# Second cross-attention: queries and keys of four heads in even and odd tiles, scores in eight parts of TensorE

## The chip, the cores and the metric

The kernel runs on one core of a Trainium2 chip. The metric is the device time in microseconds (us) of one execution. The kernel before has a median of 2383.0 us in three runs (2380.41 to 2383.2).

## The reference, cut to what matters

Two transformer blocks work on `x` (8 batches, 512 rows, 256 columns), all in float32. The change lies in the cross-attention of the second block, where 512 rows of a batch ask 64 context rows, with 16 heads of width 64:

```python
def _attn(xq, ctx, wq, wkv, wo, bo):
    q = _heads(xq @ wq)                       # 16 heads, 512 x 64 each
    k, v = jnp.split(ctx @ wkv, 2, axis=-1)   # 16 heads, 64 x 64 each
    k = _heads(k); v = _heads(v)
    q = _rope(q, sq, cq)                      # (even, odd) -> (even*c - odd*s, even*s + odd*c)
    k = _rope(k, sk, ck)
    sim = jnp.einsum('bhnd,bhmd->bhnm', q, k) * DH ** (-0.5)
    a = jax.nn.softmax(sim, axis=-1)
    o = jnp.einsum('bhnm,bhmd->bhnd', a, v)
    return o.transpose(0, 2, 1, 3).reshape(...) @ wo + bo
```

Before it come the first block (a self-attention, a cross-attention and a gated feed-forward) and the second block's self-attention over 512 rows; after it comes the second block's feed-forward.

## The kernel before, in words

The program runs in stages: the first block (three batches' pieces interleaved by `run_blocks`, a planner that places work by slots), the second block's self-attention (`slots`, pool `ph4`), the second cross-attention (`cross`, pool `ph5`) and the last feed-forward (`feed_forward`). In the last three the order on TensorE (PE), VectorE (DVE), ScalarE (ACT) and GpSimd (POOL) is the order in which the Python code issues the instructions. The DMAs of SyncE's queue (SP) are put in order by the scheduler, so their place can differ from the code's.

**Keys and values.** The keys of the second cross-attention are made during the first block: `keys1(p)` multiplies, rotates with `rope_pair` (L844 on) and `store_keys1` writes one pair of heads to the DRAM tile `k_d` by a DMA that POOL issues. Values come at the end of the self-attention stage (`cross_values`). Per batch, `load_kb` and `load_vb` fetch them to one of two sets of SBUF tiles. A tile `kb` is `[128, 8 pairs, 2, 64]`: it holds each pair of heads twice as wide as needed, the half that belongs to the other head being zero, so that one matmul with 128 rows gives the scores of two heads.

**Rope.** `rope_pair` takes a PSUM tile that holds two heads, with even and odd components in blocks of 32 partitions. DVE does one product with the cosine over 128 partitions (L849) and two with the sine over 64 partitions each, which land exchanged (L852). One POOL addition makes the turned tile `q` (L853).

**The stage around the change.** `cross` walks 8 batches `b` of 8 steps `j`. A step issues one pair's query product and rope (`queries`, three ahead: `LEAD = 3`). Steps 0, 2, 4 and 6 issue `score(b, j // 2)`: two matmuls of 128x128 weights by 512 columns into one two-bank PSUM tile `ps_S`, and one exponential of 1024 columns on ACT (L1261) that makes a tile `p` of two pairs. `sums` multiplies four pairs of `p` by a 128x32 selector[...]. ACT copies the sums (L1271), and a round trip through DRAM (L1274, L1276) lays them out for a reciprocal on DVE (`inverse`, L1281). Its result goes back through DRAM (L1283), and eight DMAs spread it over partitions as `rb` (L1288). `scaled` multiplies the four pairs of one half of the heads by `rb`, even pairs on POOL and odd ones on DVE (L1295). `outer` multiplies values with the output weights into `vw`, and `cross_out(b - 1, t)` multiplies the scaled `p` of the batch before with `vw`, pair 0 to pair 7 in that order, for rows of tile `t`. `turn` transposes the rows of the next batch, and `rows_` normalises those of the one after. PSUM tiles of `queries`, `outer`, `sums`, `turn` and `cross_out` come from one ring of four banks (`bank_x`: `D`, `O`, `X`, `X`).

**Form of matmuls.** A float32 matmul shows as two records in the trace. Where a helper issues a matmul, its line is L118. The self-attention's `score` (L1019 on) already uses heads in fours: even and odd components of four heads are in two tiles, each head having 32 partitions[...].

Of the kernel before, what the change touches and what calls it, by code (L numbers as in the profile page):

```python
# [10 lines left out]
F32 = mybir.dt.float32  # L11
# [7 lines left out]
P = 128  # L19
# [68 lines left out]
def fast_path(ctx: ExitStack, tc: tile.TileContext, a: dict, out: bass.AP):  # L88
# [28 lines left out]
    def mm(o, lhsT, rhs, start=True, stop=True):  # L117
        nc.tensor.matmul(o, lhsT, rhs, start=start, stop=stop)  # L118
# [144 lines left out]
    def load_k(dst, src, p=P):  # L263
        nc.sync.dma_start(dst, src.rearrange("(k p) f -> p k f", p=p))
# [223 lines left out]
    def at(i, fn):  # L488
        beside.setdefault(max(i, -1), []).append(fn)
# [348 lines left out]

    k_d = dram.tile([P, NPAIR, B, T], F32, name="k_d", bufs=1)
    v_d = dram.tile([P, NPAIR, B, T], F32, name="v_d", bufs=1)

    def rope_pair(wk, ps, c, sn, shape, dst):  # L844

        t1 = wk.tile([P, N], F32, tag="t1", name="t1")
        t2 = wk.tile([P, N], F32, tag="t2", name="t2")
        t1, t2 = (t[:, :].rearrange("p (j n) -> p j n", n=shape[-1]) for t in (t1, t2))
        nc.vector.tensor_tensor(t1, ps, c.to_broadcast(shape), ALU.mult)  # L849
        for i in range(2):  # L850
            src, d = slice(64 * i, 64 * i + 64), slice(64 - 64 * i, 128 - 64 * i)
            nc.vector.tensor_tensor(t2[d], ps[src], sn[src].to_broadcast([64, *shape[1:]]), ALU.mult)  # L852
        nc.gpsimd.tensor_tensor(dst, t1, t2, ALU.add)  # L853

    kv1_stack = ExitStack()
    kv1 = {}
# [1 line left out]
    def open_keys1():  # L858
        kv1["pool"] = pool = kv1_stack.enter_context(tc.tile_pool(name="kv1", bufs=2))
        kv1["w"] = w = pool.tile([96, 2, H * HD1], F32, name="w_ck", bufs=1)  # L860
        load_k(w, a["ca_wk2"], 96)
        for n in ("rope_c", "rope_s2"):
            kv1[n] = t = pool.tile([P, T], F32, name=f"t_{n}", bufs=1)
            nc.sync.dma_start(t, a[n][:, 0:T])

    def keys1(p):
        ps = bank_x()
        for k in range(2):
            mm(ps, kv1["w"][:, k, p * P : (p + 1) * P], ctxzT[:, k, :], k == 0, k == 1)
        kv1[p] = q = kv1["pool"].tile([P, N], F32, tag="q", name="q", bufs=8)  # L870
        rope_pair(kv1["pool"], ps.rearrange("p (j n) -> p j n", j=B), kv1["rope_c"][:, None, :], kv1["rope_s2"][:, None, :],
                  [P, B, T], q.rearrange("p (j n) -> p j n", j=B))

    def store_keys1(p):
        nc.gpsimd.dma_start(k_d[:, p], kv1[p].rearrange("p (b t) -> p b t", b=B))

    wk2 = wk3 = w_1 = w_3 = w_2 = None
    wpool = nk = rope_c = rope_s = w_sq = w_sk = w_sv = w_so = ready = None
# [42 lines left out]
    at(CYCLE, open_cross)  # L921
    for p in range(NPAIR):
        at(CYCLE + 2 + 2 * p, lambda p=p: keys1(p))
        at(min(CYCLE + 5 + 2 * p, 2 * CYCLE), lambda p=p: store_keys1(p))
    at(2 * CYCLE, open_ff)
    at(CYCLE * B + X1 + 3, open_block1)
    for n in range(3):
# [15 lines left out]
    kvs = []  # L943

    def kv_first():
        w = wpool.tile([P, 2, NPAIR, 2, T], F32, tag="w4", name="kv", bufs=1)
        kvs.append((w[:, 0], w[:, 1]))
        return kvs[0]

    def load_kb(b):  # L950
        for i in range(4):
            r = slice(32 * i, 32 * i + 32)
            nc.sync.dma_start(kvs[b % 2][0][r, :, i % 2, :], k_d[r, :, b, :])

    def load_vb(b):
        for e in range(2):
# [1 line left out]
            nc.sync.dma_start(kvs[b % 2][1][r, :, e, :], v_d[r, :, b, :])  # L958

    def cross_weights():  # L960
        cross.update(v=load_w("ca_wvp", 1, 96), o=load_w("ca_wo", 2), q=load_w("ca_wq2", 0),
                     s=load_table("rope_s2", "s"))

    def cross_values(wk, p):
        ps = bank_x()
# [7 lines left out]
    with tc.tile_pool(name="ph4", bufs=2) as wk:  # L973
# [8 lines left out]
        def batch4(b):  # L982
# [115 lines left out]
            if b:  # L1098

                pieces = normed_in_pieces(nk, b, EPS1, lambda z: s.update(z=z))  # L1100
                last(base - 8, pieces[0])
                last(base - 6, pieces[1])
                after[base - 6] = [pieces[2]]
                last(base - 5, lambda: add_row(b, row("sabo")))
                after.setdefault(base - 4, []).append(turn)
                last(base - 3, lambda: queries(0))
                last(base - 2, lambda: values(0, (0, 1)))
                last(base - 2, lambda: keys(0))
                last(base - 1, lambda: values(0, (2, 3)))
            else:  # L1110
                s["hT"] = ready

                def begin():
                    queries(0)
                    add_row(0, row("sabo"))
                    both = bank_s()
                    keys(0, (both[:, 0, :], both[:, 1, :]))
                    values(0, (0, 1))

                last(-1, begin)  # L1120

                after[-1] = [lambda: values(0, (2, 3))]
                last(4, lambda: [nc.gpsimd.memset(z, 0.0) for z in (kb, vb)])
                last(5, lambda: load_kb(0))
            for h in range(2):
                last(base + h, lambda h=h: values(1, (2 * h, 2 * h + 1)))
# [70 lines left out]
        with tc.manual_schedule(engines={ENG.PE, ENG.DVE, ENG.Activation, ENG.Pool}):  # L1197
            slots()

    w_co, w_cq, rope_s2, ready = cross["o"], cross["q"], cross["s"], first_rows[1]  # L1200

# [1 line left out]
    with tc.tile_pool(name="ph5", bufs=2) as wk:  # L1205
        w_f1 = load_w("ff_w1", 1)
        w_f2 = load_w("ff_w2", 3)
        kvs.append(tuple(wk.tile([P, NPAIR, 2, T], F32, name=n, bufs=1) for n in ("kb", "vb")))


        turned_rows = {0: ready, 1: first_rows[2]}
# [30 lines left out]
            nc.scalar.copy(s["vw"][:, 2 * pp : 2 * pp + 2, :], ps.rearrange("p (i d) -> p i d", i=2))  # L1242

        def queries(n):
            b, p = divmod(n, NPAIR)
            if b == B:
                return
            ps = bank_x()
            for k in range(2):
                mm(ps, w_cq[:, k, p * P : (p + 1) * P], turned_rows[b][:, k, :], k == 0, k == 1)  # L1250
            ss[b][p] = q = wk.tile([P, N], F32, tag="q", name="q", bufs=7)
            rope_pair(wk, ps[:, None, :], rope_c[:, None, :], rope_s2[:, None, :], [P, 1, N], q[:, None, :])

        def score(b, pp):
            s = ss[b]
            ps = bank_s()
            for i in range(2):
                p = 2 * pp + i
                mm(ps[:, i, :], kvs[b % 2][0][:, p, :, :].rearrange("p e k -> p (e k)"), s[p])
            s["p", pp] = pr = wk.tile([P, 2, N], F32, tag="p", name="p", bufs=8)  # L1260
            nc.scalar.activation(pr, ps, AF.Exp, scale=HD1 ** -0.5)  # L1261

        def sums(b, half):

# [86 lines left out]
            return good  # L1351

        def cross():
            LEAD = 3
            for n in range(LEAD):
                queries(n)
                if n:
                    outer(0, n - 1)
            for z in kvs[1]:
                nc.gpsimd.memset(z, 0.0)  # L1360
            for b in range(B):
                for j in range(NPAIR):
                    if j % 2 == 0:
                        queries(NPAIR * b + j + LEAD)
                        score(b, j // 2)
                    if b and j in (5, 6):
                        cross_out(b - 1, j - 4)
                    if j % 2:
                        queries(NPAIR * b + j + LEAD)
                    if j < 2:  # L1370
                        for pp in (2 * j, 2 * j + 1) if b else (2 + j,):
                            outer(b, pp)
                    if b:
                        if j == 0:
                            scaled(b - 1, 0)
                        if j == 1:
                            inverse(b - 1, 1)
                        if j == 3:
                            scaled(b - 1, 1)
                    if j == 3:  # L1380
                        turn(b + 1)
                    if b:
                        if j == 7:
                            cross_out(b - 1, 3)
                    if j == 2 and b + 1 < B:
                        load_kb(b + 1)
                        load_vb(b + 1)
                    if j == 4:
                        sums(b, 0)
                        if b:  # L1390
                            cross_out(b - 1, 0)
                    if j > 4:
                        rows_(b + 2, j - 5)
                    if j == 6:
                        inverse(b, 0)
                    if j == 7:
                        sums(b, 1)

        def feed_forward():
            good = top = None  # L1400
# [803 lines left out]
def _layout(inputs):  # L2204
# [24 lines left out]

    arr["ca_wv"] = l1["ca_wkv"][:, H * HD1 :].reshape(CD, 8, 2, HD1).transpose(0, 2, 1, 3).reshape(CD, H * HD1)  # L2230

    def both_apart(w):
        return w.reshape(w.shape[0], NPAIR, 2, HD1 // 2, 2).transpose(0, 1, 4, 2, 3).reshape(w.shape[0], H * HD1)

    arr["ca_wq2"], arr["ca_wk2"] = both_apart(l1["ca_wq"]), both_apart(l1["ca_wkv"][:, : H * HD1])
    def fours(w):
        return w.reshape(w.shape[0], H // 4, 4, HD1 // 2, 2).transpose(0, 1, 4, 2, 3).reshape(w.shape[0], H * HD1)

    arr["sa_wq4"], arr["sa_wk4"] = fours(l1["sa_wq"]), fours(l1["sa_wkv"][:, : H * HD1])
    arr["ca_wvp"] = l1["ca_wkv"][:, H * HD1 :]  # L2240

    cols = np.zeros((P, NCOL), f)

# [23 lines left out]
    arr["rope_c"] = np.concatenate([cos] * 4, axis=0)  # L2267
    arr["rope_s"] = np.concatenate([sin, -sin] * 2, axis=0)
    arr["rope_s4"] = np.concatenate([sin] * 4, axis=0)
    arr["rope_s2"] = np.concatenate([sin, sin, -sin, -sin], axis=0)  # L2270
    return {k: np.ascontiguousarray(v, dtype=f) for k, v in arr.items()}


# [14 lines left out]
```

## Time and profile before

| What | Value |
|---|---|
| median of three runs | 2383.0 us |
| span of the profiled execution | 2378.6 us |
| PE busy in it | 2361.7 us, 99% of the span |
| DVE, ACT, POOL busy | 1141.8, 886.8, 958.6 us |
| second cross-attention, from its first query product to the last feed-forward's first matmul | 1815.4 to 2131.9 us of the span |
| PE stretches of its batches 2 to 5 | 41.13 us each |

Busy times are sums over one engine, idle time is what is left, and the wait shown with an instruction is the idle time of its engine just before it. The profiled execution's span is 4.4 us less than the median of the three runs: that is what lies around the first and last instruction, and run-to-run spread. On a timeline of PE, the records of one matmul start about 0.43 us apart where they have 512 columns. The shown length of a group is longer by the modelled end of its last record, so the distance between two starts is read, not the length.

### The profile page before, as it was taken

The page shows a single profiled execution, that of the slowest core. Times are in us where ns is not written, and L with a number is a line of the kernel's source. Part 1 is how long each engine was busy: PE and PEld are TensorE (multiplying, and loading weights), DVE is VectorE, ACT ScalarE, POOL GpSimd, SP SyncE. Part 2 cuts the span into 40 slices and gives each one's busy share as a digit, 9 for nine tenths or more (in the row PEclk, how much of TensorE's full clock was granted, in tenths as well). Part 3 has the DMA queues.
Part 4 walks back from the last instruction along what each step waited for, and adds up shares of the span by engine and source line. Part 5 has one row for each costly group of instructions (what it writes and reads, how often), then busy time and mean ns, then how long its engine had stood idle before and what let it go on. Part 6 is the DMA issues. An engine that isn't in the chain of part 4 may idle for free.

```text
span 2378.6 us, 28548 instructions
## 1 busy us (share of the span) xinstructions
PE 2361.7 (99%) x10964; PEld 1153.9 (49%) x10964; DVE 1141.8 (48%) x2115; ACT 886.8 (37%) x1118; POOL 958.6 (40%) x588
## 2 busy tenths in 40 slices
PE   9999999999999999999999999999999999999999
PEld 4333544544545633434444444444345566667666
DVE  4564544534335345555454555545445767651110
ACT  4665545555542134333333333333332222221221
POOL 4563223323201046555555555555543545441110
PEclk9999999999999999999999999999999999999999
DMA  5130000000002001000000000000123222210000
GB/s 186 38 104 11 17 15 13 16 15 6 13 11 93 1 1 33 10 26 12 19 19 19 19 19 20 19 19 19 37 59 103 74 65 69 65 59 28 18 23 20
DMA packets 84897, 84.07 MB, mean 35 GB/s; under 512 B 42656, under 2 KB 59792, under 8 KB 84752
## 3 DMA queue, kind: packets, MB, share of 16 engines
q1 hardware_dynamic: 83208, 78.99, 10.8%
q8 instruction: 88, 1.44, 0.2%
q0 software_dynamic: 640, 2.10, 0.2%
q10 hardware_dynamic: 904, 1.07, 0.1%
q14 instruction: 57, 0.47, 0.1%
HBM read 72.09 MB, written 10.04 MB: 35 GB/s over the span
## 4 chain that ended last, share of the span: by engine, by line
PE 96%; DMA 1%; DVE 1%; issue 1%; ACT 1%; POOL 0%; SPq 0%; DVEq 0%; ACTq 0%; POOLq 0%
PE ps_X L118 39%; PE ps_S L118 24%; PE ps_D L118 16%; PE ps_O L118 14%; PE ps_X L429 1%; DMA rb<-rec 1%; PE ps_X L616 1%; PE ps_X L576 0%; ACT p L596 0%; DMA rec<-rec 0%; PE ps_D L616 0%; PE ps_D L429 0%; POOL var L567 0%; PE ps_D L576 0%; ACT den L1063 0%
## 5 line engine op out<-in xcount | busy, mean ns | idle before, releaser
L118 PE MATMUL ps_S<-q,k 32*128 32x512 f32 (+1 forms) x3072 | 416.3, 622 | 2.5 <-ACT p L596 1.5
L1028 ACT ACTIVATE p<-ps_S 128x1024 f32<-128x1024 f32 x256 | 248.4, 1021 | 449.5 <-PE ps_S L118 449.2
L596 ACT ACTIVATE p<-ps_S 128x1024 f32<-128x1024 f32 x256 | 248.2, 1022 | 197.5 <-PE ps_S L118 196.8
L118 PEld LDWEIGHTS ps_S<-q,k 32*128 32x128 f32 (+1 forms) x3072 | 141.5, 183 | 228.0 <-issue 161.5
L1047 DVE TENSOR_TENSOR sm<-sm,p 128x1024 f32<-128x1024 f32 x128 | 251.8, 2026 | 0.3 <-issue 0.2
L1010 POOL TENSOR_TENSOR q<-t 128x512 f32<-128x512 f32 x32 | 59.7, 1866 | 327.8 <-DVE t L1008 286.8
L1007 DVE TENSOR_TENSOR t<-ps_X,rope_c 128x512 f32<-128x512 f32 x126 | 86.9, 690 | 211.2 <-PE ps_X L118 211.2
L184 POOL TENSOR_TENSOR rstd<-rstd,mhalf 128x4 f32<-128x4 f32 x49 | 50.1, 1023 | 329.4 <-DVE rstd L183 328.1
L853 POOL TENSOR_TENSOR q<-t,t 128x512 f32<-128x512 f32 x72 | 94.9, 1318 | 154.8 <-DVE t L852 151.7
L567 POOL TENSOR_TENSOR var<-var,mhalf 128x32 f32<-128x32 f32 (+1 forms) x17 | 87.4, 5140 | 170.1 <-DVE var L561 169.9
L1043 POOL TENSOR_TENSOR sm<-p 128x1024 f32<-128x1024 f32 x64 | 149.9, 2370 | 1.8 <-ACT p L1028 1.8
L118 PE MATMUL ps_X<-hT,w 128*128 128x512 f32 x328 | 150.5, 597 | 0.0
L1093 POOL TENSOR_TENSOR oT<-oT,rb 128x512 f32<-128x512 f32 x63 | 126.7, 2029 | 29.2 <-DMA rb<-rec_d 29.2
L118 PE MATMUL ps_O<-p,v 128*64 128x512 f32 x512 | 134.9, 605 | 0.0
L118 PE MATMUL ps_D<-p,v 128*64 128x512 f32 x512 | 131.6, 592 | 0.0
L118 PE MATMUL ps_O<-p,h 128*32 128x512 f32 x1024 | 130.4, 610 | 0.8 <-ACT p L596 0.8
L118 PE MATMUL ps_X<-w_sa_wv,hT 128*128 128x512 f32 x256 | 118.3, 605 | 0.0
L118 PE MATMUL ps_X<-hT,w_sa_wq 128*128 128x512 f32 x256 | 115.9, 595 | 0.0
L118 PE MATMUL ps_X<-w_sa_wo,oT 128*128 128x256 f32 x512 | 113.9, 381 | 0.6 <-DVE t L1008 0.5
L118 PE MATMUL ps_X<-hT,w_sa_wk 128*128 128x512 f32 x248 | 113.2, 599 | 0.0
L118 PE MATMUL ps_S<-hT,w_ff_w 128*128 128x512 f32 x256 | 111.3, 592 | 0.0
L466 DVE TENSOR_TENSOR x<-ps_X,x 128x512 f32<-128x512 f32 x27 | 18.7, 691 | 190.5 <-PE ps_X L118 190.5
(283 smaller groups left out, 3619.4 us busy)
## 6 DMA issues: line engine op xcount, KB each, us to landing
rb<-rec SPq DMA_DIRECT2D x128, 128.0 KB
rb<-rec_d SPq DMA_DIRECT2D x124, 128.0 KB
rb<-rec SPq DMA_DIRECT2D x16, 256.0 KB
out_dram<-x SPq DMA_DIRECT2D x15, 256.0 KB
x<-in_x_dram SPq DMA_DIRECT2D x7, 512.0 KB
gate<-modd SPq DMA_DIRECT2D x24, 128.0 KB
k_d<-q POOLq DMA_DIRECT2D x8, 256.0 KB, 2.4
v_d<-v SPq DMA_DIRECT2D x8, 256.0 KB
```

The source lines that it names most:

```text
L118: nc.tensor.matmul(o, lhsT, rhs, start=start, stop=stop)
L184: nc.gpsimd.tensor_tensor(r[:, :n], r[:, :n], mhalf[:, :n], ALU.pow)
L429: nc.tensor.transpose(ps[:, t * P : (t + 1) * P], z[:, t, k * P : (k + 1) * P], ident)
L567: nc.gpsimd.tensor_tensor(var, var, half, ALU.pow)
L596: nc.scalar.activation(pr[u], pss[u], AF.Exp, scale=HD0 ** -0.5)
L853: nc.gpsimd.tensor_tensor(dst, t1, t2, ALU.add)
L1007: nc.vector.tensor_tensor(c, ps, rope_c, ALU.mult)
L1010: nc.gpsimd.tensor_tensor(r[0], ec, os, ALU.subtract)
L1028: nc.scalar.activation(pr, pss[u], AF.Exp, scale=HD1 ** -0.5)
L1043: nc.gpsimd.tensor_tensor(sm, s["p", g, 0, u], s["p", g, 1, u], ALU.add)
L1047: nc.vector.tensor_tensor(s["sm", g, u], s["sm", g, u], s["p", g, t, u], ALU.add)
L1093: eng.tensor_tensor(o, o, s["rb", g, u], ALU.mult)
```

## The change

Queries and keys are now made for four heads at a time. For each group `g` of four heads there are an even and an odd product (`e`), each with its 32 components of four heads in 128 partitions. `rope_half` does two DVE products over 128 partitions for each; after the odd one, POOL makes the two turned tiles by a subtraction and an addition. `kb` has half the size, no zeros, and takes one DMA in place of four. `score(b, half)` takes eight heads at once: sixteen matmuls of 32 rows and 64 weight columns in four row by two column parts, into two `ps_S` tiles, followed by two exponentials. A tile column of `p` now holds two heads that are four places apart, and value and output weights are reordered to match. The order of `cross` is changed: `LEAD` is 5; scores come at steps 0 and 4; the sums of a half come right ahead of the scores of the next; `turn`, `inverse(b - 1, 1)` and `scaled(b - 1, 1)` move to steps 2, 2 and 4, and the four `cross_out` of a batch to steps 5, 6 and 7. The buffers of the rope's products (`t`) are five, those of `q` eight.

```diff
-    def rope_pair(wk, ps, c, sn, shape, dst):
...
-        nc.vector.tensor_tensor(t1, ps, c.to_broadcast(shape), ALU.mult)
-        for i in range(2):
-            src, d = slice(64 * i, 64 * i + 64), slice(64 - 64 * i, 128 - 64 * i)
-            nc.vector.tensor_tensor(t2[d], ps[src], sn[src].to_broadcast([64, *shape[1:]]), ALU.mult)
-        nc.gpsimd.tensor_tensor(dst, t1, t2, ALU.add)
+    def rope_half(pool, s, key, e, ps, c, sn, shape, bufs, dst):
...
+        s["t", key, e] = tc_, ts = tile(), tile()
+        nc.vector.tensor_tensor(shaped(tc_), ps, c.to_broadcast(shape), ALU.mult)
+        nc.vector.tensor_tensor(shaped(ts), ps, sn.to_broadcast(shape), ALU.mult)
+        if e:
+            (ec, es), (oc, os) = s.pop(("t", key, 0)), s.pop(("t", key, 1))
+            d = dst()
+            nc.gpsimd.tensor_tensor(d[0], ec, os, ALU.subtract)
+            nc.gpsimd.tensor_tensor(d[1], es, oc, ALU.add)
...
-    def store_keys1(p):
-        nc.gpsimd.dma_start(k_d[:, p], kv1[p].rearrange("p (b t) -> p b t", b=B))
+    def store_keys1(g):
+        nc.gpsimd.dma_start(k_d[:, g], kv1[g].rearrange("p e (b t) -> p e b t", b=B))
...
-        for i in range(4):
-            r = slice(32 * i, 32 * i + 32)
-            nc.sync.dma_start(kvs[b % 2][0][r, :, i % 2, :], k_d[r, :, b, :])
+        nc.sync.dma_start(kvs[b % 2][0], k_d[:, :, :, b, :].rearrange("p g e t -> p (g e) t"))
...
-        def score(b, pp):
+            rope_half(wk, ss[b], g, e, ps[:, None, :], rope_c[:, None, :], rope_s[:, None, :], [P, 1, N], 5, dst)
+
+        def score(b, half):
             s = ss[b]
-            ps = bank_s()
-            for i in range(2):
-                p = 2 * pp + i
-                mm(ps[:, i, :], kvs[b % 2][0][:, p, :, :].rearrange("p e k -> p (e k)"), s[p])
-            s["p", pp] = pr = wk.tile([P, 2, N], F32, tag="p", name="p", bufs=8)
-            nc.scalar.activation(pr, ps, AF.Exp, scale=HD1 ** -0.5)
+            pss = [bank_s() for _ in range(2)]
+            for e in range(2):
+                for j in range(4):
+                    r = slice(32 * j, 32 * j + 32)
+                    for i in range(2):
+                        g = 2 * half + i
+                        mm(pss[j // 2][64 * i : 64 * i + 64, j % 2, :], kvs[b % 2][0][r, 2 * g + e, :], s[g][e][r, :],
+                           e == 0, e == 1)
+            for u in range(2):
+                s["p", 2 * half + u] = pr = wk.tile([P, 2, N], F32, tag="p", name="p", bufs=8)
+                nc.scalar.activation(pr, pss[u], AF.Exp, scale=HD1 ** -0.5)
...
         def cross():
-            LEAD = 3
+            LEAD = 5
...
                 for j in range(NPAIR):
-                    if j % 2 == 0:
-                        queries(NPAIR * b + j + LEAD)
-                        score(b, j // 2)
-                    if b and j in (5, 6):
-                        cross_out(b - 1, j - 4)
-                    if j % 2:
-                        queries(NPAIR * b + j + LEAD)
-                    if j < 2:
-                        for pp in (2 * j, 2 * j + 1) if b else (2 + j,):
+                    if j == 0 and b:
+                        sums(b - 1, 1)
+                    if j == 4:
+                        sums(b, 0)
+                    if j % 4 == 0:
+                        score(b, j // 4)
+                    if j == 2:
+                        turn(b + 1)
+                    queries(NPAIR * b + j + LEAD)
+                    if b and j < 2:
+                        for pp in (2 * j, 2 * j + 1):
                             outer(b, pp)
                     if b:
                         if j == 0:
                             scaled(b - 1, 0)
-                        if j == 1:
+                        if j == 2:
                             inverse(b - 1, 1)
-                        if j == 3:
+                        if j == 4:
                             scaled(b - 1, 1)
-                    if j == 3:
-                        turn(b + 1)
-                    if b:
-                        if j == 7:
-                            cross_out(b - 1, 3)
+                        if j > 4:
+                            for t in ((0,), (1,), (2, 3))[j - 5]:
+                                cross_out(b - 1, t)
...
-                    if j == 4:
-                        sums(b, 0)
-                        if b:
-                            cross_out(b - 1, 0)
...
-                    if j == 7:
-                        sums(b, 1)
+            sums(B - 1, 1)
```

## The prediction

> **What bounds the kernel now.** I read the page first: busy time, then the chain of work that ended last.
>
> ```profile
> PE 2361.7 (99%) x10964; PEld 1153.9 (49%) x10964; DVE 1141.8 (48%) x2115; ACT 886.8 (37%) x1118; POOL 958.6 (40%) x588
> ...
> PE 96%; DMA 1%; DVE 1%; issue 1%; ACT 1%; POOL 0%; SPq 0%; DVEq 0%; ACTq 0%; POOLq 0%
> ```
>
> PE sets the end nearly alone. A change pays if it takes PE time away without making PE wait. The view by windows says the same of the changed stage; each window is one batch of the cross-attention:
>
> ```profile
> 1931.35:1972.48 41.13, 41.13 (x156) 25.30 (x152) 26.77 (x50) 8.94 (x12) 19.74 (x14) 1.00 0.24 68
> 1972.48:2013.61 41.13, 41.13 (x156) 25.30 (x152) 27.95 (x50) 8.94 (x12) 19.76 (x14) 1.00 0.23 67
> ```
>
> Columns: length, then busy time of PE, weight loads, DVE, ACT and POOL. PE never idles, though DVE and POOL are far from full. The timeline of PE in the second of them gives the prices (start, length, records):
>
> ```profile
> 1972.48 1.99 PE L118 MATMUL ps_X<-hT,w_ca_wq 128*128 128x512 f32 x4
> 1974.30 1.88 PE L118 MATMUL ps_S<-q,kv 128*128 128x512 f32 x4
> 1976.02 1.03 PE L118 MATMUL ps_X<-w_ca_wo,kv 128*128 128x256 f32 x4
> ...
> 1988.93 1.88 PE L118 MATMUL ps_S<-q,kv 128*128 128x512 f32 x4
> 1990.74 1.07 PE L118 MATMUL ps_O<-p,sel 128*32 128x512 f32 x8
> 1991.74 0.48 PE L118 MATMUL ps_X<-vw,p 128*128 128x256 f32 x1
> ```
>
> A score of four heads runs from 1974.30 to 1976.02: 1.72 us, four records at 0.43. The self-attention's scores show what row parts do:
>
> ```profile
> 1506.12 1.03 PE L118 MATMUL ps_D<-p,v 128*64 128x512 f32 x4
> 1507.08 2.00 PE L118 MATMUL ps_S<-q,k 32*128 32x512 f32 x16
> 1509.01 3.27 PE L118 MATMUL ps_X<-hT,w_sa_wk 128*128 128x512 f32 x7
> ```
>
> Sixteen records take 1.93 us: four rounds of four side by side, 4 x 0.43 = 1.72, and 0.21 for entering and leaving the form. The first line's four records need 0.86, two at a time, so column parts overlap too.
>
> [...] in the third fence the sums' two rounds (0.86) start 0.09 late (1988.93 + 1.72 = 1990.65), last 1.00, and the matmul after them is 0.10 longer (1.98 where 1.88 is usual), 0.33 in all. Eight parts at once appear in no row of before. [...] POOL's rope addition takes 1.26 alone, 1.71 beside DVE's scaling.
>
> **The change part by part.** Units are us; all sums are against the profiled span.
>
> *Scores.* Per half batch, before: two groups, 2 x 1.72 = 3.43. After: 16 matmuls, 32 records; in eight parts four rounds, 1.72. Sixteen halves: 16 x 1.716 = **27.5 less**. If only the four row parts overlap, it is eight rounds and nothing is saved.
>
> *Mode changes.* Before, each `sums` costs 0.33 in and out. After, sums and scores stand together: three changes in place of two. From 0.33 / 2 and the self-attention's 0.21 plus 0.10 before it, I take 0.18 each, 0.54 in place of 0.33: **3.3 more** over 16 halves, between 0 and 6.
>
> *Rope.* DVE does two products of 0.69 where it did three: 64 x 0.69 = 44 of DVE time off the path. POOL does the same number of operations, but in twos after the odd product. This delays the even tile, which before was finished alone. For the keys in the first block it is the same trade, 8 tiles, with 4 stores on POOL's queue for 8; hidden behind PE, I take 0; uncovered, a pair's second POOL operation would be 1.3 late four times, 5 at most.
>
> *Loads and zeros.* One DMA for four, one memset less: 0, under a whole batch of PE work; uncovered, a 64 KB issue is 0.6.
>
> *The moved scaling.* Now the waits. In the built order of the changed kernel, POOL in step 4 does the two operations of the query pair 8b+8 and 8b+9, and only then `p` 4 and 6 of the batch before. PE has one query product (1.72) and `cross_out`'s pairs 0 to 3 (4 x 0.43 = 1.72) between query 8b+9 and the matmul of pair 4: a cover of 3.44. These are the rows of before that price the chain (DVE, then POOL):
>
> ```profile
> 1983.18 0.69 DVE L849 TENSOR_TENSOR t<-ps_D,rope_c 128x512 f32<-128x512 f32 x1 [0.65 <-PE ps_D L118]
> ```
>
> ```profile
> 1976.74 1.71 POOL L853 TENSOR_TENSOR q<-t,t 128x512 f32<-128x512 f32 x1 [0.74 <-DVE t L852]
> 1978.41 2.94 POOL L1295 TENSOR_TENSOR p<-p,rb 128x512 f32<-128x512 f32 x2
> 1981.97 1.26 POOL L853 TENSOR_TENSOR q<-t,t 128x512 f32<-128x512 f32 x1 [0.62 <-DVE t L852]
> ```
>
> The query that feeds the DVE row begins at 1981.19 and is done by cadence at 1982.91; DVE starts 0.27 later. Two products are 1.40, the hand to POOL 0.15, two POOL operations 2.53, `p` 4 between 1.26 and 1.71, 0.08 back: 5.7 to 6.1. PE stands 2.3 to 2.7. Pair 6 follows 1.26 to 1.71 later, when PE has needed only 0.86 for pairs 4 and 5: 0.4 to 0.85 more. I take 3.1; with the second row's 1.71 also on the pair's first operation 3.9, without any contention 2.65. Batches 1 to 6: 6 x 3.1 = **18.6**, 16 to 23. [...] Before, the scaling came a whole step earlier, with 7.2 of PE work as its cover.
>
> In the last batch there are no more queries, so less covers `rb`. From its last query: DVE 1.7 and reciprocal 0.35; the DMA out issued and landed (1982.24 to 1984.42 in SP's rows) 2.2; two `rb` issues at 0.6; about 2.6 to land (1986.80 to 1989.53); POOL 1.5: 9.5. PE reaches pair 4 at about 7.2, and the later pairs trail `rb`'s issues by 1.2 each. **4.6**, between 3 and 6.
>
> *Waits of the scores.* `score(b, 1)` needs query 8b+7, two steps earlier. Even tile: 0.27 + 1.40 + 0.15 + 1.26 + 0.08 = 3.16; cover: one query and the sums, 1.72 + 1.27 = 2.99; wait 0.18. The odd tile is 1.26 later, the even half of the scores lasts 0.86: 0.4. **4.1** for seven batches; **2.3** for the eighth, whose step 3 has no query; about **1.2** for `score(1, 0)`, where the first batch's steps are bare queries and POOL's pairs with five `t` buffers turn slower (4.2 a pair) than PE asks (3.4). Between 4 and 9 in all.
>
> *A wait for a bank.* In batch 1 the reciprocals of batch 0 come late and DVE's scaling holds up the rope, which holds a bank. Before has 0.73 of this, which goes. **2.4**, between 0 and 4: at step 2, the transposes.
>
> Sum: -27.5 + 3.3 + 18.6 + 4.6 + 7.6 + 2.4 - 0.7 = **+8.3**, a span of 2386.9. The median of the runs lies 4.4 above the profiled span, so 2391.3; I say **2391.5**.
>
> **The rivals.** *Faster.* The mechanism is the cover in step 5: POOL's chain decides. If PE's waits stay below 24.9 in all (27.5 - 3.3 + 0.7), the change gains; that is where the scaled pair is worth under about 2.4 a batch with the rest small. With POOL uncontended (7 x 2.65 = 18.6) and the score and bank waits lost in slack, it ends 6.3 lower: 2377. For it: DVE is under 70% busy. Against it: the order of POOL is fixed and each link has a measured length. *Half the parts.* Column parts don't add to row parts: no 27.5, while part of the score waits goes; about 31 more than now, 2414. Against it: the self-attention has both forms, each overlapping fully. *Longer waits.* POOL and DVE collide at every pair, all POOL operations at 1.7, edges dear: 23 + 6 + 9 + 4 + 6 - 28.2 = 20 more: 2403. *It doesn't do what it says*: the built order shows the sixteen small matmuls, so only the half-parts case remains of that.
>
> **How the numbers follow.** Likeliest (0.57): 2383 to 2397, with 0.12 inside the 0.2% (4.8 us) that a measurement of this kernel tells from no change. Longer waits 0.15, half the parts 0.08, short waits 0.20, of which 0.14 faster by over 0.2%. Slower: 0.45 + 0.15 + 0.08 = 0.68; same: 0.12 + 0.06 = 0.18; faster 0.14. The range 2377 to 2405 leaves out the half-parts case and the far end of the faster one.
>
> **What would show it.** In the profile after: score records at 32*64, sixteen pairs in about 1.9; a batch near 42 where it was 41.13; PE idle near 3 before the fifth matmul of `cross_out` tile 0, released by POOL's scaling; small idles in scores released by POOL's rope. If PE stays gapless there, I am wrong and it gains; if scores take 3.6 a half, the parts don't overlap.

## The result, and the profile after

| Kernel | Median (runs) | Lowest to highest | Ratio to before, 95% |
|---|---|---|---|
| before | 2381.7 us (4) | 2380.36 to 2383.2 | |
| after | 2396.0 us (4) | 2394.51 to 2397.98 | 1.0061 [1.0049, 1.0074] |

The change costs 14.3 us, 0.6%; the prediction said 2391.5. The profiled execution of after has a span of 2396.4 us, 17.8 more than that of before. All times are in us. First the same two lines of the page as before: busy times, then the chain of work that ended last.

```profile
PE 2356.0 (98%) x11348; PEld 1146.4 (48%) x11348; DVE 1079.1 (45%) x2043; ACT 885.4 (37%) x1118; POOL 953.4 (40%) x582
...
PE 94%; issue 2%; POOL 1%; DMA 1%; DVE 1%; ACT 1%; SPq 1%; POOLq 0%; ACTq 0%; DVEq 0%
```

PE is busy 5.7 less than before and the span is 17.8 longer: it now idles 23.5 more. DVE has lost 62.7, and nothing came of that.

Where is the time? The first query product of the second cross-attention starts at 1816.68 (before 1815.41) and the last feed-forward at 2149.56 (before 2131.85). So the stage went from 316.4 to 332.9, **16.4 more**; what stands ahead of it gave 1.3, and the tail nothing. The 1.3 says little: in the profiles of the changed kernel and of its eight variants below, which are the same up to this stage, the stage starts anywhere between 1814.0 and 1819.2. Two batches of the stage by windows (length; busy PE, weight loads, DVE, ACT, POOL; granted clock; DMA):

```profile
1938.18:1980.10 41.92, 39.13 (x202) 23.57 (x201) 20.51 (x41) 8.74 (x12) 19.88 (x14) 1.00 0.23 66
1980.10:2023.61 43.51, 40.73 (x202) 24.52 (x201) 20.91 (x41) 8.74 (x12) 19.91 (x14) 0.96 0.22 63
```

Two things are to be seen against before's 41.13, 41.13 busy. PE idles 2.79 in the first and 2.78 in the second. And the second batch has 1.6 more *busy* time than the first for the same work, at a clock of 0.96. The timeline of PE in the first of them (start, length, records, idle before):

```profile
1938.18 1.07 PE L118 MATMUL ps_O<-p,sel 128*32 128x512 f32 x8
1939.17 1.97 PE L118 MATMUL ps_S<-q,kb 32*64 32x512 f32 x32
1941.07 1.98 PE L118 MATMUL ps_X<-hT,w_ca_wq 128*128 128x512 f32 x4
...
1953.46 2.50 PE L118 MATMUL ps_S<-q,kb 32*64 32x512 f32 x32
1955.90 1.98 PE L118 MATMUL ps_O<-hT,w_ca_wq 128*128 128x512 f32 x4
...
1963.56 1.13 PE L118 MATMUL ps_X<-vw,p 128*128 128x256 f32 x4 [2.23 <-POOL p L1314]
1965.24 1.13 PE L118 MATMUL ps_X<-vw,p 128*128 128x256 f32 x4 [0.55 <-POOL p L1314]
1966.21 1.88 PE L118 MATMUL ps_D<-hT,w_ca_wq 128*128 128x512 f32 x4
```

A half's scores take 1.90 from start to start (1939.17 to 1941.07), where two groups of before took 3.43. The 32 records start in four rounds of eight (from 1939.17, 1939.65, 1940.08 and 1940.51, each round's eight within 0.05), so all eight parts work at once. The half in step 4 takes 2.44: 0.54 of waiting for the rope is spread in it. Then PE waits 2.23 for pair 4 of `cross_out` and 0.55 for pair 6, both released by POOL's scaling. POOL's rows at that time:

```profile
1959.35 1.26 POOL L858 TENSOR_TENSOR q<-t 128x512 f32<-128x512 f32 x1 [4.55 <-DVE t L854]
1960.58 1.71 POOL L859 TENSOR_TENSOR q<-t 128x512 f32<-128x512 f32 x1
1962.25 2.94 POOL L1314 TENSOR_TENSOR p<-p,rb 128x512 f32<-128x512 f32 x2
```

POOL stood idle for 4.55, then did the query pair (2.90), then the scaling. This is the chain that the prediction priced, link by link. What it did not have is what follows the waits. Windows of 2 us in batch 2, where the waits end at 1919.96 and 1921.63; the granted clock is the third number from the end:

```profile
1919.00:1921.00 2.00, 1.04 (x4) 0.68 (x4) 1.86 (x3) 0.00 (x0) 2.00 (x2) 1.00 0.49 108
1921.00:1923.00 2.00, 1.45 (x4) 1.17 (x4) 1.53 (x6) 0.00 (x0) 0.58 (x1) 0.67 0.00 0
1923.00:1925.00 2.00, 2.00 (x4) 1.01 (x3) 0.00 (x0) 0.00 (x0) 0.00 (x0) 0.50 0.00 0
1925.00:1927.00 2.00, 2.00 (x8) 1.27 (x7) 0.79 (x2) 0.00 (x0) 0.00 (x0) 0.98 0.00 0
```

After the idle PE runs at half clock (0.50) for 3.41: the four records behind the second wait take 1.87 (1921.63 to 1923.50), where the same four take 0.97 at full clock in the batch above (1965.24 to 1966.21). That costs 1.7 here (a batch of 43.61 against 41.92) and is booked as busy. It happens in batches 2, 4 and 6, not in 3 and 5, once more in batch 1, and for longer (6.83) in the last one, whose waits are these:

```profile
2124.42 2.34 PE L118 MATMUL ps_S<-q,kb 32*64 32x512 f32 x30 [0.80 <-POOL q L858]
...
2130.98 0.70 PE L118 MATMUL ps_D<-vw,p 128*128 128x256 f32 x2 [2.29 <-POOL p L1314]
2132.04 0.70 PE L118 MATMUL ps_D<-vw,p 128*128 128x256 f32 x2 [0.36 <-DVE p L1314]
2134.27 7.45 PE L118 MATMUL ps_D<-vw,p 128*128 128x256 f32 x20 [1.54 <-POOL p L1314]
```

Twenty records of 256 columns take 7.29 to the next start, where they need 4.30.

### The profile page after: what moved, and what is told of

Read it like the earlier page. It is cut to its first block, busy times and chain, and to the rows that moved or that the text cites. A ratio compares the mean times of both kernels' runs of the same rounds, so it can differ in the third digit from the quotient of the medians.

```text
span 2396.4 us, 29139 instructions
## 1 busy us (share of the span) xinstructions
PE 2356.0 (98%) x11348; PEld 1146.4 (48%) x11348; DVE 1079.1 (45%) x2043; ACT 885.4 (37%) x1118; POOL 953.4 (40%) x582
## 3 DMA queue, kind: packets, MB, share of 16 engines
q10 hardware_dynamic: 904, 1.07, 0.1%
## 4 chain that ended last, share of the span: by engine, by line
PE 94%; issue 2%; POOL 1%; DMA 1%; DVE 1%; ACT 1%; SPq 1%; POOLq 0%; ACTq 0%; DVEq 0%
PE ps_X L118 39%; PE ps_S L118 23%; PE ps_D L118 16%; PE ps_O L118 14%; PE ps_X L429 1%; DMA rb<-rec 1%; POOL p L1314 1%; PE ps_X L616 1%; SPq L1307 0%; PE ps_X L576 0%; ACT p L596 0%; DMA rec<-rec 0%; PE ps_D L616 0%; POOL var L567 0%; PE ps_D L429 0%
## 5 line engine op out<-in xcount | busy, mean ns | idle before, releaser
L118 PEld LDWEIGHTS ps_X<-w_sa_wo,oT 128*128 128x128 f32 x512 | 96.1, 190 | 22.8 <-issue 5.3
```

## The experiments

My theory: the scores gain what was forecast, and waits of order eat it, most of all POOL's scaling behind the query pair; each wait can also bring a stretch at half clock. The rivals: the eight parts don't give 27.5, or they themselves lower the clock; the DMA of `rb` and not POOL's order holds pair 4; PE takes matmuls in strict order so that the order of the parts matters. All kernels are the changed kernel with the edit shown. The first four shared runs of before with a median of 2380.43 (16 runs), the last four with 2379.62 (9 runs).

**Pairs 4 and 6 ahead of the query pair on POOL.**

```diff
-        def scaled(b, half):
+        def scaled(b, half, js=range(4)):
...
+                    if b and j == 4:
+                        scaled(b - 1, 1, (0, 2))
                     queries(NPAIR * b + j + LEAD)
...
-                            scaled(b - 1, 1)
+                            scaled(b - 1, 1, (1, 3))
```

> In step 4 POOL scales pairs 4 and 6 before it makes the two rope tiles of the odd query, in place of after them; DVE's order, the parts of the scores and all else are as in the changed kernel. Theory (POOL's order makes the wait): the wait of 2.23 + 0.55 us ahead of pairs 4 and 6 in cross_out falls under 0.5 in batches 1 to 6, and with it the stretches at a granted clock of about 0.6; about 25 us less than the changed kernel, near 2371. Rival (the wait is for the spread reciprocals, rb, that SP brings): POOL stands before the scaling as long as before, and the time stays within 4 us of 2396. Rival (the form changes and small matmuls cost it): unchanged, 2396.

Measured: 2379.7 (2376.19 to 2384.83, 12 runs), ratio 0.9993 [0.9983, 1.0004]; the stage takes 313.05, 19.8 less than after. One batch by windows, and what is left of its wait, with the row of POOL that releases it:

```profile
1933.33:1972.76 39.43, 38.98 (x201) 23.56 (x200) 19.46 (x41) 8.74 (x12) 19.49 (x14) 1.00 0.23 69
```

```profile
1957.79 1.25 PE L118 MATMUL ps_X<-vw,p 128*128 128x256 f32 x4 [0.45 <-POOL p L1314]
```

```profile
1956.47 1.27 POOL L1314 TENSOR_TENSOR p<-p,rb 128x512 f32<-128x512 f32 x1 [1.63 <-DMA rb<-rec]
```

The clock is 1.00 with the same eight-part scores, so the parts don't lower it. POOL's place in line was the cause of most of the wait in batches 1 to 6. What is left of it has another cause: POOL now stands idle until a DMA brings `rb`, 1.63 in the row above, and batch 5 keeps waits of 0.90 and 1.07 that way. So the rival named `rb` holds for the rest. The expectation was 25 less than after; the mean span fell by 16.6, of which 12.1 is work and waiting and 4.5 clock (by the table near the end). The score waits, the bank wait of batch 1 (1.92) and the last batch's waits (2.03 and 1.07, where there is no query pair to overtake) stayed. Half clock followed in batch 1 and in the last batch: behind the bank wait eight records take 5.23 (1863.49 to 1868.72) where 3.53 is usual, and from 2090 to 2135, with the last batch in it, the mean clock is 0.96.

**The reciprocal of the second half a step earlier.**

```diff
-                        if j == 2:
+                        if j == 1:
                             inverse(b - 1, 1)
```

> inverse(b - 1, 1) is issued in step 1 in place of step 2, so that rb is spread a step earlier; the order on POOL stays. Theory (POOL's order): rb was in time already, the waits stay at 2.2 + 0.5 us, the time within 4 us of 2396; only the last batch, where rb counts, gets about 2 shorter. Rival (rb is what is late): the waits go, about 2371.

Measured: 2389.65 (2388.15 to 2392.73, 5 runs), ratio 1.0039 [1.0025, 1.0053]; the stage takes 325.44, 7.4 less than after, where about 2 was expected. A wait of batches 1 to 6:

```profile
1961.98 2.36 PE L118 MATMUL ps_X<-vw,p 128*128 128x256 f32 x8 [2.56 <-POOL p L1314]
1964.17 1.88 PE L118 MATMUL ps_D<-hT,w_ca_wq 128*128 128x512 f32 x4
```

The wait for pair 4 stays, so `rb` wasn't its cause there; in the last batch only 0.26 is left of 4.19, so there it was. Nearly all of the gain lies there: from its first sums to the feed-forward the last batch takes 33.24 in place of 40.57, as the half-clock stretch behind its waits (3.0) went with them: the clock is 1.00 from 2100 to 2140. A batch at full clock takes 41.79 in place of 41.92. One wait is shown where after has two, but the eight records behind it take 2.19 (1961.98 to 1964.17) where 1.72 is usual, so pair 6 still costs a part.

**The column parts in turn.** Same matmuls; all eight of the first column part are issued ahead of the second's.

```diff
-            for e in range(2):
-                for j in range(4):
-                    r = slice(32 * j, 32 * j + 32)
-                    for i in range(2):
+            for i in range(2):
+                for e in range(2):
+                    for j in range(4):
+                        r = slice(32 * j, 32 * j + 32)
```

> The sixteen matmuls of a half are issued so that the first column part's eight come before the second's: at most four row parts work side by side, as in the self-attention; all else as in the changed kernel. Theory (eight parts overlap in the changed kernel): scores go from 1.9 us to about 3.6 a half, 27 us over 16 halves, less some 4 of score waits that get more cover: 2416 to 2424. Rival (row and column parts don't add up, the gain came from elsewhere): no change, 2396.

Measured: 2396.82 (2395.47 to 2398.76, 4 runs), ratio 1.0067 [1.0051, 1.0084]: no difference from after. **A miss.** A half's scores:

```profile
1938.24 2.00 PE L118 MATMUL ps_S<-q,kb 32*64 32x512 f32 x32
1940.17 1.98 PE L118 MATMUL ps_X<-hT,w_ca_wq 128*128 128x512 f32 x4
```

1.93 from start to start. If the second column part could begin only with the first part's second products, 0.86 in, a half would take 3 x 0.86 = 2.6 (an estimate from 0.43 a record, two records a product; the 3.6 of the expectation took the two parts wholly one after the other). The 1.93 is below both, so the second column part did not wait for the matmuls issued ahead of it in the first. What lets it start wasn't tried. The edit was meant to take the overlap of eight parts away and didn't, so it doesn't decide between theory and rival; the 1.90 of a half does.

**Filling the wait.** Two matmuls of 512 columns that nobody reads (0.86 each) stand ahead of pair 4, not in batches 1 to 6 only, as the expectation has it: the condition in the edit holds in the last batch too. The work done is otherwise the same.

```diff
         def cross_out(b, t):
+            if t == 0 and b < B - 1:
+                s = ss[b]
+                s["ps"], fill = bank_x(), bank_x()
+                for k in range(8):
+                    if k == 4:
+                        for _ in range(2):
+                            mm(fill, w_cq[:, 0, 0:P], turned_rows[b + 2 if b + 2 < B else b + 1][:, 0, :])
+                    mm(s["ps"][:, 0:D], s["p", k // 2][:, k % 2, 0:P], s["vw"][:, k, :], k == 0, k == 7)
+                return
```

> Two matmuls of 128 x 512 that nobody reads (1.7 us of PE work) are put into the wait ahead of pair 4 in batches 1 to 6; they take one more bank of the ring. The chain on POOL is unchanged, so the end of a wait is not moved. Theory (idle PE lowers the granted clock afterwards): idle falls to about 0.5 + 0.55 us, the stretches at a clock of 0.6 go in batches 1, 2, 4 and 6, about 7 us less than the changed kernel, near 2389. Rival (the lower clock has another cause, or the long records after a wait are only modelled so): the time stays at 2396 or grows by what the filling adds.

Measured: 2392.6 (2386.99 to 2395.78, 4 runs), ratio 1.0052 [1.0036, 1.0069]: 3.4 less than after, where some 7 were expected. The profiled execution is the fastest of them, 2386.99; two of its batches:

```profile
1933.70:1975.62 41.92, 40.85 (x206) 24.32 (x205) 20.45 (x41) 8.74 (x12) 19.90 (x14) 1.00 0.24 66
1975.62:2017.54 41.92, 40.82 (x205) 24.32 (x204) 19.98 (x41) 8.74 (x12) 19.92 (x14) 1.00 0.20 57
```

In batches 1 to 6, 10.3 of idle time (6 x 1.72) became work, the batch stays at 41.92, and the half-clock stretches are gone (the clock is 1.00 in each of seven windows from 1860 to 2150): the stage takes 323.45, 9.4 less than after. But its other three runs have mean clocks of 0.995 to 0.997, where this one has 0.999, and spans of 2389.6 to 2394.2. There is no trace of those, so where their clock fell isn't known; before, whose stage has no such waits, also ranges from 0.995 to 0.999 from run to run.

**One matmul of fill, and a longer wait.** The first is the edit above with one matmul. In the second, POOL does four additions of 128 columns, read by nobody, ahead of the scaling:

```diff
+                            junk = wk.tile([P, P], F32, tag="junk", name="junk", bufs=1)
+                            for _ in range(4):
+                                nc.gpsimd.tensor_tensor(junk, ss[b - 1]["p", 2][:, 0, 0:P], ss[b - 1]["p", 2][:, 1, 0:P], ALU.add)
                             scaled(b - 1, 1)
```

> The changed kernel with one unread matmul of 128x512 (0.86) ahead of pair 4 of the output product in batches 1 to 6, where two were put in before: the first wait should fall from 2.23 to 1.4, the second stays 0.55. Theory A (any idle of over 1 us lowers the granted clock): half clock still follows in every other batch, stretches alternate by 1.6. Theory B (it takes over some 2 us in a few us): clock 1.00 in each batch, batches of 41.9 each, as with two matmuls. Time about 2394 under A, 2389 under B.

> The changed kernel with four additions of 128x128 on POOL ahead of the scaling in step 4, read by nobody, to make PE's wait longer by an estimated 1.6 (0.4 each), 3.8 in place of 2.23. Theory A (the clock falls with the length of the idle): the half clock follows in every batch, not in every other, and lasts as long or longer, so batches take about 45 each and the time is near 2396 + 7 x 1.6 + 3 x 1.7 = 2412. Theory B (what decides is where the wait falls in a fixed period of the clock's control): some batches with it, some without, in another pattern; about 2407.

Measured, one run each: 2393.96 and 2409.32. Two batches of the first (waits 1.38 and 0.55), then two of the second (a wait of 4.41, in batch 2 with 0.29 behind it):

```profile
1895.98:1937.90 41.92, 40.00 (x204) 24.00 (x203) 20.82 (x41) 8.74 (x12) 19.89 (x14) 1.00 0.22 68
1937.90:1981.50 43.60, 41.68 (x203) 24.94 (x202) 20.42 (x41) 8.74 (x12) 19.91 (x14) 0.96 0.21 64
```

```profile
1895.34:1940.64 45.30, 40.60 (x201) 24.34 (x201) 20.34 (x41) 8.74 (x12) 21.80 (x18) 0.96 0.22 60
1940.64:1985.50 44.86, 40.45 (x202) 24.63 (x201) 20.33 (x41) 8.74 (x12) 21.79 (x18) 0.96 0.22 62
```

With 1.9 of idle the clock still falls in every other batch; with 4.4 it falls in each of batches 2 to 6 (0.96, in one 0.93). The patterns are those that theory A forecast. Its rule for the first, any idle of over 1, can't be right: batches 2, 4 and 6 have the same waits at full clock. And the second doesn't rule out its theory B, a fixed period of the clock's control, as a wait longer than the period would hit it in every batch. The trace of after decides this below.

**The second half of the value products in step 3**, as a cover for the score's wait.

```diff
-                    if b and j < 2:
-                        for pp in (2 * j, 2 * j + 1):
+                    if b and j in (0, 3):
+                        for pp in (0, 1) if j == 0 else (2, 3):
                             outer(b, pp)
```

> The changed kernel with one edit: the second half of the products of values and output weights moves from step 1 to step 3, ahead of the score that waits for the rope. My theory (the score's wait is a lack of cover of 0.54, and of some 1.9 in the last batch): score waits gone, the scaling's waits unchanged, so 7 x 0.54 + 1.5 = 5 less than the changed kernel, about 2391; a little less again if the clock stays up. Rival (the wait moves on to the fifth matmul of the output product, because POOL sets the pace): the scaling's wait grows by 0.5 a batch and the time stays at 2396.

Measured: 2392.85 (2390.32 to 2394.33, 4 runs), ratio 1.0053 [1.0037, 1.0068]: 3.2 below after where 5 was expected. The score's wait is gone in batches 1 to 6 and down to about 0.5 in the last. The wait for pair 4 is 2.56 to 2.69, and no second one is shown, but the eight records behind it take 2.2 in place of 1.72; batches at full clock take 41.25 to 41.39, 0.5 to 0.7 less than after's 41.92. So the waits for pairs 4 and 6 cost in sum what they did, and the score's wait didn't move on to them. The bank wait of batch 1 grew to 2.72. At full clock the gain is 6.4 (2375.6 against 2382.0, by the table near the end), and about half of it was lost again by a lower mean clock, 0.9935 over four runs where after has 0.9948.

**All three edits of order.** Pairs 4 and 6 first, the early reciprocal and the late value products.

> The changed kernel with three edits of order: pairs 4 and 6 scaled on POOL ahead of step 4's query pair, the reciprocal of the second half one step earlier (step 1), and the second half of the products of values and output weights in step 3, between the last query and the score that needs it. My theory (the scores' gain of 27.5 is real, and was eaten by waits of order and by the clock after them): the score waits (0.54 in seven batches, 1.9 in the last), the last batch's waits (3.9) and most of what the first of these edits left (0.5 a batch) go, so from that run's span of 2377.8 about 11 less, a span near 2367 and a median near 2369, ratio 0.995 to the kernel before; clock 1.00 in every window. Rival 1 (the gain never was 27.5, mode changes eat it): it stays at 2378 to 2380, with PE gapless. Rival 2 (the waits move on: with less PE work in step 1, the reciprocal holds DVE and the transposes wait for a bank): 2374 to 2382, with idle of 1 to 2 at step 2 of every batch.

Measured: **2361.23** (2358.94 to 2366.04, 5 runs), ratio **0.9923 [0.991, 0.9937]**: 18.4 faster than before, 35 faster than after, and 8 below the expectation. The profiled execution happens to be the slowest of the five (span 2363.6); two of its batches and its largest idle:

```profile
1894.87:1932.94 38.07, 38.07 (x201) 23.48 (x200) 20.35 (x41) 8.83 (x12) 19.88 (x14) 1.00 0.25 72
1932.94:1971.01 38.07, 38.07 (x202) 23.49 (x201) 20.34 (x41) 8.83 (x12) 19.85 (x14) 1.00 0.25 72
```

```profile
1865.79 3.51 PE L118 MATMUL ps_O<-hT,w_ca_wq 128*128 128x512 f32 x4 [2.72 <-DVE t L854]
```

In batches 2 to 6 PE is gapless again, at full clock, and a batch takes 3.06 less than before. The expectation counted 5.2 of waits in those five batches of the first experiment (5 x 1.04); by its trace they held 8.3, most of the surplus in batch 5, and the mean clock rose by 0.001, which is 2.4. That is 5.5 of the 8. Eight batches make 24.5 where the prediction's first two terms make 24.2 (27.5 - 3.3). The rival "the gain never was 27.5" falls. The rival "waits move on to a bank" holds once, in batch 1, and there the four records behind the wait take 3.30 (1865.79 to 1869.09) where 1.72 is usual.

## Why the prediction was right, and what it lacked

The sum by its own steps, forecast against what the profiled executions show for the stage. The clean batch of the last experiment tells waits and work apart. One correction is needed for that: the idle time shown is less than what a wait costs. In the batch of after, 1963.56 to 1965.24 is 1.68, for four records (0.86) and 0.55 of shown idle; 0.27 is missing. With 0.27 for each wait the batch lengths come out: 38.07 + 0.54 + 2.23 + 0.55 + 2 x 0.27 = 41.93 against 41.92 measured, and 38.07 + 0.54 + 0.86 + 1.38 + 0.55 + 0.54 = 41.94 against 41.92 with one matmul of fill. Both sides of a wait show it: the end of the last record is put 0.17 behind the point where the next would start in a stream (four records of 256 columns are 1.03 long, with the next 0.86 later), and the four records after a wait are 1.13 long. What takes the time isn't shown.

| Step | Forecast | Measured | From |
|---|---|---|---|
| scores and mode changes | -27.5 + 3.3 | -24.5 | 8 x (41.13 - 38.07) |
| waits for pairs 4 and 6, batches 1 to 6 | 18.6 | 19.1 | 2.23 + 0.27, then 5 x (2.78 + 0.54) |
| the same, last batch | 4.6 | 5.0 | 4.19 + 3 x 0.27 |
| waits of the scores | 7.6 | 6.5 | 7 x 0.54, 2.2 in the last batch, 0.5 for `score(1, 0)` |
| bank in batch 1 | 2.4 | 2.2 | 1.91 + 0.27 |
| before's own wait | -0.7 | -0.7 | |
| half clock after waits | not there | 9.5 | 4.8 in batches 2, 4 and 6, 1.7 in batch 1, 3.0 in the last |
| sum | +8.3 | +17.1 | stage: +16.4, so 0.7 is counted too much |

**The mechanism and each priced wait were right.** Eight parts overlap in full, rope work taken from DVE gained nothing, POOL's order ate the gain, and each term was within about 1 us. PE did nothing else in the 2.23: the query product issued behind the waiting matmuls starts at 1966.21, after them. Two readings in it are a little off, without weight: the matmul after the sums is 1.99 long in its third fence, where the text has 1.98, and 1986.80 to 1989.53 is 2.7, where it took 2.6.

**The term that was missing is the clock.** The prediction took PE's time per record as fixed after a wait. The waits that it forecast came to 3.1 for one of the batches 1 to 6 and to 4.6 for the last, and it put nothing for the clock at either. In the trace of after the granted clock falls to 0.50 five times in the stage, from 1877.29, 1921.66, 2006.99, 2092.33 and 2133.29: 13, 25, 25 and 12 times 3.413 apart. The first four stretches last 3.413, the fifth 6.827. The two stretches ahead of the stage, from 71.64 and 92.12, are 6 times 3.413 apart, and 1877.29 comes 523 times 3.413 after the second. In the trace of before the three stretches (71.49, 91.97 and 2375.49) are 6 and 669 times 3.413 apart. Cut into windows of this length that end where the stretches begin, PE's wait in batch 2 (first two rows) and in batch 3 (last three rows) looks like this:

```profile
1918.25:1921.66 3.41, 1.16 (x5) 0.70 (x5) 2.52 (x4) 0.00 (x0) 3.33 (x3) 1.00 0.38 87
1921.66:1925.07 3.41, 3.41 (x6) 2.16 (x7) 0.87 (x4) 0.00 (x0) 0.00 (x0) 0.50 0.00 0
1959.21:1962.62 3.41, 2.12 (x9) 1.33 (x7) 1.11 (x2) 0.00 (x0) 3.27 (x3) 1.00 0.55 181
1962.62:1966.04 3.42, 1.93 (x8) 1.40 (x9) 3.42 (x7) 0.00 (x0) 2.57 (x2) 1.00 0.25 55
1966.04:1969.45 3.41, 3.41 (x14) 2.25 (x13) 1.38 (x3) 0.00 (x0) 0.00 (x0) 1.00 0.02 5
```

In batch 2 most of the wait falls into one window, which holds 1.16 of PE work, and the next window is at half clock. In batch 3 the same wait is split over two windows, with 2.12 and 1.93 of work, and the clock stays. Two batches together are 85.4 to 85.5, 25.0 windows, so the pattern repeats every two batches. A whole idle window isn't needed. Between 200 and 2362 us the trace of after has 627 such windows at full clock. Five hold 1.13 to 1.40 of PE work (as the profile shows it), and half clock followed each of them. The least of the other 622 holds 1.61 (from 1860.22, in batch 1), and half clock followed none. The window from 2133.29, itself at half clock, holds 2.43, and another at half clock followed. The 633 windows of before hold 2.69 or more, and half clock followed none.

The loss to the clock also shows without any window. The product of span and mean granted clock is what the work would take at full clock (an estimate: the clock has three decimals, and 0.001 of it is 2.4):

| Kernel | Runs | Mean span | Mean clock | Product, mean of the runs |
|---|---|---|---|---|
| before | 16 and 9 | 2379.2 and 2377.7 | 0.9976 and 0.9982 | 2373.5 and 2373.5 |
| after | 4 | 2394.6 | 0.9948 | 2382.0 |
| pairs 4 and 6 first | 12 | 2378.0 | 0.9966 | 2369.9 |
| early reciprocal | 5 | 2388.2 | 0.9950 | 2376.2 |
| two matmuls of fill | 4 | 2390.4 | 0.9968 | 2382.7 |
| late value products | 4 | 2391.1 | 0.9935 | 2375.6 |
| all three edits | 5 | 2359.7 | 0.9976 | 2354.0 |

After stands 8.5 above before at full clock, which is the forecast's +8.3; the other 6.9 of 15.4 in span is clock. Filling the wait with two matmuls changes the product by 0.7 and the clock by 0.002, as it should if it only takes idle away; part of that difference in clock comes from the fastest of its four runs.

**The offset.** The prediction added 4.4 to the span for the median. A run's time is 1.4 to 2.8 above its own span in the runs here; the rest of the 4.4 was spread between runs of before. The forecast was so some 2.5 too high in this term, and by luck that hid part of the missing clock: without it, it would have said 2389.

**The rivals.** *Faster* named the point that decides, waits below 24.9 in all; they came to 19.1 + 5.0 + 6.5 + 2.2 = 32.8. *Half the parts* and *it doesn't do what it says* are out by the 1.90 of a half. *Longer waits* (2403) is the case that the end of the sum moved toward, but by the clock and not by contention: POOL's rows are 1.26 and 1.71 as assumed.

What stays open: where the clock fell in the three untraced runs with two matmuls of fill, and what happens between 1.40 and 1.61 of work, where after has no window at full clock. Why the start of the stage moves by up to 5.2 between profiles with the same work ahead of it isn't known either. Part of it is clock: after, which starts the stage at 1816.68, has 6.8 at half clock ahead of it, while in all three edits, which start it at 1819.22, the page puts the second of 40 slices of the span under 0.9 of full clock, where after's has 0.9 or more in each.

## What to carry to other kernels

When work is taken from the engine that sets the end, ask first whether what feeds it still comes in time: here an engine that was 40% busy cost most of the gain, because a scaling stood behind two operations that nobody needed yet. Moving it ahead of them brought the time back to that of before, and two other moves that add no work made it 0.8% faster than before. A wait of TensorE cost its shown idle time and 0.27 more here, and a batch in which half clock followed was 1.5 to 1.7 longer again (43.46 to 43.61 against 41.92): price both. Compare span times granted clock when two kernels differ by less than a per cent.

## What the runs showed of the hardware that I had not expected

- Half clock after short idles: in after, waits of 2.23 + 0.55 us brought a stretch at 0.50 in batches 2, 4 and 6 and none in 3 and 5. The windows of 3.413 us just ahead of the stage's stretches hold 1.13 to 1.40 us of PE work, the other windows at full clock between 200 and 2362 us 1.61 or more. With one matmul of fill, 1.38 + 0.55 brought it in two of batches 2 to 6 (clock 0.96 in batches 3 and 5); a single 2.56 with the early reciprocal in three of six windows (0.96); 4.41 with the longer wait in each of batches 2 to 6 (0.96, once 0.93). The stretches of after's stage last 3.41, the last one 6.83.
- A wait costs about 0.27 more than the idle shown: 1.68 from start to start, where four records (0.86) and the idle shown (0.55) make 1.41.
- A half's scores take 1.90 with the column parts interleaved and 1.93 with all of the first column part issued ahead of the second; held to that order it would be 2.6 (the estimate above).
- Eight parts of 32 rows by 64 columns do 32 records of 512 columns in 1.90 from start to start, against 3.43 for the same scores in full-size matmuls.
